# Moving the z projection of two images into the first image's scan, with a round trip through DRAM

## The chip, the cores and the metric

The kernel runs on one core of a Trainium2 chip. The metric is the device time of one execution in microseconds (us). The engines are named as in the profile: PE (TensorE, with PEld for its weight loads), DVE (VectorE), ACT (ScalarE), POOL (GpSimd), and SP, whose queue issues nearly all DMAs.

## The reference

Four layers work on `x` of shape (4 images, 384 channels, 48 x 48). Each is `x + layer(group_norm(x))`. Layer 0 is a state-space block, and it is the one that the change is about:

```python
xz = xs @ in_proj_w.T                      # 2304 tokens of an image, 384 -> 2 x 768
xin, z = jnp.split(xz, 2, axis=-1)
xin = silu(causal_conv4(xin) + conv_b)
dt, Bm, Cm = split(xin @ x_proj_w.T)       # 24, 16, 16
dt = softplus(dt @ dt_proj_w.T + dt_proj_b)
h = exp(dt * A) * h_prev + dt * B * x      # for each of 768 channels and 16 states
y = (sum over states of h * C + xin * D) * silu(z)
out = layer_norm(y @ out_proj_w.T)
```

Layer 1 is a projection, an 8 x 8 spectral filter, a depthwise 3 x 3 convolution and a gated projection; layer 2 a depthwise 11 x 11 convolution built from 4 points; layer 3 a mixture of 4 experts with a gate.

## The kernel before, in words

**Tiles.** Layer 0 runs image by image (b = 0 to 3), and an image's 2304 tokens in 5 chunks of 460 or 464 (t). So there are 20 chunks `i`. Channels lie on the 128 partitions: 384 are 3 tiles, 768 are 6 (m or j). A chunk has 96 (channel tile, state) pairs, and each is one **slot** `u`: 1920 slots in all. In each slot ACT makes `da = exp(dt * A)` in PSUM (`decay`, L821), POOL makes `bu = u * B` (`drive`, L832), DVE runs the scan along the tokens (L845), DVE or POOL multiplies by C (L865 or L874: in image 0 one slot in three is POOL's, later every other pair), and PE adds the result into a PSUM bank by a transposing matmul (`turned`, L770). ACT copies the scan's last column into `carry` (L859) for the next chunk. B and C rows come from DRAM, spread over all partitions, by two DMAs for every second slot, on SP's queue, in rings of 3 and 4 buffers; `drive` runs 3 slots ahead of the scan and `decay` 2.

**The work beside the scan.** The order of instructions on each engine is written out by this loop. Other work is cut into tasks, Python generators that yield the engine of their next step; a `Lane` advances each of its active tasks by at most one step when it comes by (once for ACT steps and once for the others in each slot; after an ACT step the task waits for the next slot). A task starts when the tasks it needs have ended, and a lane's queue is first in, first out. A `Meter` adds up the PE time that tasks announce: a slot takes 2.3 us off it and adds 0.44 for its own transposes, and while it stands above 2.0 a bound lane starts no step with a weight.

- Lane `aux` (not bound) holds layer 0's own tasks, put there for each chunk by `plan`: output projection (`out`, L916) and layer norm of the chunk before; `project_z` (six tasks j, L674 and L682, from slot 30 of the chunk); `project` for the next chunk (L642, L655, L661); `gates`, the Silu of `xc` and `z` in one go (slot 64); `steps` (dt); the image's group norm for the next image: `image_stats` (loads of half a channel tile and three `bn_stats` each, L573, in the first three chunks), `image_norm`, and `fold` (loads `w_inx` or `w_inz`, scales its rows by 1/std on ACT, and makes the mean's contribution on PE, L598).
- Lane `one` holds layers 1 to 3's routing scores of the image before (`later`, from slot 42 of an image on), and lane `two` the experts of that image (`experts`, L1602, 64 blocks of two products for an image), which need the last task of `later`. So image 0's scan has neither beside it. What is left after the scans runs in a tail: `later` of image 3, the rest of the experts, the routing and all experts of image 3 (L1702, L1719).

**z.** `project_z(i, j)` multiplies the chunk's `x` by the folded `w_inz` into a PSUM bank of the ring `mm` (3 banks), and ACT adds the bias and writes `zs[:, j]` (one buffer for all six j). `gates` applies Silu, `gate` (L902) multiplies y into it, and `out_proj` reads it.

**PSUM.** 8 banks: `mm` 3, `y` 2, `da` 2, `acc` 1. The bank `acc` is used by layers 1 and 2 only, so image 0's scan does not use it.

The functions that the diff touches:

Of the kernel before, what the change touches and what calls it, by code (L numbers as in the profile page):

```python
# [16 lines left out]
P = 128  # L17
NB, C, H, W = 4, 384, 48, 48
HW = H * W
# [114 lines left out]
def wait(slots):  # L134
    for _ in range(slots):
        yield ("pool",)
# [3 lines left out]
def tile_layers(ctx: ExitStack, tc: tile.TileContext, a: dict, out: bass.AP):  # L140
# [272 lines left out]
    with ExitStack() as first:  # L413
# [138 lines left out]
        def now(steps):  # L552
            for _ in steps:
                pass

        def scans(wk, mm, ring, meter, place, lanes, begin):
# [23 lines left out]


            def fold(b, which):
                w = (w_inx, w_inz)[which]
# [82 lines left out]
            def project_z(i, j):  # L666
                (b, t), c = G[i], st[i]
                n, d = CHUNKS[t], batch[b]
                yield ("pe", 2.3, (ring, 1))
                if "zs" not in c:  # L670
# [145 lines left out]
            def decay(u):  # L816
                i, p, m, s, _ = where(u)
                (b, t), c = G[i], st[i]
                n = CHUNKS[t]
                da = live["da", u] = mm.tile([P, 512], F32, name=f"da{b}_{t}_{m}_{s}", tag="da")  # L820
                nc.scalar.activation(  # L821
                    da[:, :n], c["dt", p][:, m % 2, :n], AF.Exp, scale=a_neg[:, m, s : s + 1]
                )
# [151 lines left out]

            aux = Lane(1 << 30, meter, bound=False)
            named = {}

            def plan(i, at):
# [3 lines left out]
                def put(q, name, make, *needs):  # L983
                    task = Task(make, [named[k] for k in needs if k in named], at + q)
                    named[name] = task
                    todo.append((q, task))
# [14 lines left out]
                if i < len(G):  # L1001
# [23 lines left out]
                    if b + 1 < NB:  # L1025
                        if t < CT:
                            put(43, ("stats", b, t, 0), lambda: image_stats(b + 1, t, 0), *rest)
                            put(66, ("stats", b, t, 1), lambda: image_stats(b + 1, t, 1),
                                ("stats", b, t, 0))
                        if t == CT:  # L1030
                            put(48, ("mean", b + 1), lambda: image_norm(b + 1))
                            put(70, ("fold", b + 1, 0), lambda: fold(b + 1, 0),
                                ("mean", b + 1), *done)
                        if t == CT + 1:
                            put(54, ("fold", b + 1, 1), lambda: fold(b + 1, 1), *done[:MT])
                aux.queue.extend(task for _, task in sorted(todo, key=lambda x: x[0]))

            def ready(u):
# [3 lines left out]
                while task and not task.ended:  # L1042
# [4 lines left out]
                    assert n < 1000, "stuck"  # L1047

            now(fold(0, 0))
            now(fold(0, 1))  # L1050
# [7 lines left out]
            with tc.manual_schedule():  # L1058
# [6 lines left out]
                spread(3, 0)  # L1065
                for u in range(2):
                    decay(u)
                for u in range(N + 6):
                    if u % LEN == 0 and u <= N:
                        plan(u // LEN, u)  # L1070
                    if u < N and u % (LEN * NC) == 42 and u > 42:
                        begin(G[u // LEN][0])
                    place[0] = u
                    for lane in (aux, *lanes):
                        lane.step(True, u)
# [7 lines left out]
                    meter.slot(0.44)  # L1083
                    early = u % PAIR >= 8
                    if early:
                        add(u - 5, True)
                        add(u - 3, False)
                    for lane in (aux, *lanes):
                        lane.step(False, u)
                    if u < N:  # L1090
                        product_now(u)
                    if u + 2 < N:
                        decay(u + 2)
                    if 0 < u <= N:
                        product(u - 1)
                    if u + 3 < N:
                        ready(u + 3)
                        drive(u + 3)
                    if not early:
                        add(u - 5, True)  # L1100
                        add(u - 3, False)
# [835 lines left out]
```

## Time and profile before

| what | value |
|---|---|
| median of 4 runs (lowest, highest) | 5428.84 us (5424.33, 5430.86) |
| the profiled execution's own time | 5433.5 us |
| its span (first to last instruction) | 5431.6 us |
| busy: PE, DVE, ACT, POOL | 4670.4, 4056.4, 2986.5, 3364.1 us |
| mean granted clock of PE | 0.912 |
| scan of image 0 (slots 0 to 479) | 89 to 1025 us |
| scan of image 1, 2, 3 | to 2140, to 3350, to 4528 us |
| tail | 4528 to 5432 us |
| chunk 0 to 4 | 179, 190, 188, 192, 187 us |
| chunk 14, chunk 19 (the last of images 2 and 3) | 221, 213 us |
| POOL's waits for B or C from DRAM: image 0, 1, 2, 3 | none listed, 8, 21, 25 us |

The borders of the scans are the starts of the 1st, 481st, 961st and 1441st scan instruction (L845). "Busy" is the union of an engine's instructions; an fp32 matmul shows as two records, so z's 18 matmuls of a chunk column block (6 groups j of 3) make 36 records. A wait line reads: who waited, for whom, us in total, how often, longest.

### The profile page before, as it was taken

How to read it: one execution, taken by the hardware profiler on the slowest of the kernel's cores; microseconds unless marked ns; L12 is line 12 of the kernel's file. 1: busy time of each engine (PE TensorE's matmuls, PEld its weight loads, DVE VectorE, ACT ScalarE, POOL GpSimd, SP SyncE). 2: the span in 40 equal slices, each digit the busy share in tenths (PEclk: the TensorE clock that was granted, in tenths of full speed). 3: DMA queues.
4: the chain of work that ended last, by engine and by line, in shares of the span. 5: the costliest groups of instructions: out<-in, count | busy, mean ns of one | idle time of the engine just before them, and what ended most of it. 6: DMA issues, size and time to landing. Idle time of an engine off the chain costs nothing. (4 is left out here: it accounts for less than half of the span.)

```text
span 5431.6 us, 81808 instructions
## 1 busy us (share of the span) xinstructions
PE 4670.4 (86%) x27796; PEld 3680.4 (68%) x27796; DVE 4056.4 (75%) x5581; ACT 2986.5 (55%) x6632; POOL 3364.1 (62%) x3020
## 2 busy tenths in 40 slices
PE   5677677687678989988889999988899999999899
PEld 3445455454447777665668887765678878889799
DVE  5989989888998888899887778899977774452200
ACT  3555565565558755655467655655576753334321
POOL 3878778876678788766667678776777673000000
PEclk8887788798789999999899999999999999999899
DMA  4444444454345555644555556554556554543200
GB/s 121 137 138 142 125 130 144 125 154 128 107 128 148 147 156 169 174 147 141 153 166 172 152 165 179 156 148 135 171 159 170 159 170 147 161 140 113 63 27 23
DMA packets 628392, 758.95 MB, mean 140 GB/s; under 512 B 58870, under 2 KB 622182, under 8 KB 627583
## 3 DMA queue, kind: packets, MB, share of 16 engines
q1 hardware_dynamic: 617668, 751.98, 47.5%
q8 instruction: 221, 3.62, 0.3%
q10 hardware_dynamic: 10298, 1.67, 0.2%
q14 instruction: 205, 1.67, 0.1%
HBM read 663.81 MB, written 89.65 MB: 139 GB/s over the span
## 5 line engine op out<-in xcount | busy, mean ns | idle before, releaser
L832 POOL TENSOR_TENSOR bu<-u,B 128x460 f32<-128x460 f32 (+1 forms) x1920 | 2224.9, 1168 | 809.5 <-DVE g L845 422.2
L821 ACT ACTIVATE da<-dt,a_neg 128x460 f32<-128x460 f32 (+1 forms) x1920 | 1242.9, 649 | 288.9 <-DVE g L865 185.0
L770 PE MATMUL y<-ident,g 128*115 128x128 f32 (+1 forms) x7680 | 1145.4, 298 | 272.4 <-DVE g L865 166.0
L770 PEld LDWEIGHTS y<-ident,g 128*115 128x115 f32 (+1 forms) x7680 | 1015.5, 187 | 500.1 <-DVE g L865 200.8
L874 POOL TENSOR_TENSOR g<-g,C 128x460 f32<-128x460 f32 (+1 forms) x885 | 1030.8, 1165 | 249.9 <-ACT carry L859 237.6
L845 DVE TENSOR_TENSOR_SCAN da<-da,carry,bu 128x460 f32<-128x460 f32 (+1 forms) x828 | 971.6, 1173 | 123.1 <-ACT da L821 95.3
L845 DVE TENSOR_TENSOR_SCAN g<-da,carry,bu 128x460 f32<-128x460 f32 (+1 forms) x708 | 820.0, 1167 | 106.0 <-ACT da L821 41.7
L865 DVE TENSOR_TENSOR g<-da,C 128x460 f32<-128x460 f32 (+1 forms) x1035 | 654.1, 632 | 89.5 <-PE y L770 28.5
L859 ACT COPY carry<-da 128x1 f32<-128x1 f32 x828 | 130.6, 158 | 834.3 <-DVE g L865 831.2
L1602 PE MATMUL pout<-hr,we 128*128 128x144 f32 x3456 | 484.7, 296 | 40.9 <-ACT hr L1618 30.8
L1602 PEld LDWEIGHTS pout<-hr,we 128*128 128x128 f32 x3456 | 456.3, 197 | 64.2 <-ACT hr L1618 41.7
L1602 PE MATMUL ph<-xe,we 128*128 128x144 f32 x3456 | 473.2, 292 | 12.8 <-DMA xe<-x3d 6.9
L1602 PEld LDWEIGHTS ph<-xe,we 128*128 128x128 f32 x3456 | 449.9, 195 | 29.5 <-issue 9.3
L1409 PE MATMUL pc<-band,row 128*128 128x162 f32 (+14 forms) x3456 | 457.0, 286 | 6.3 <-ACT row L1396 6.0
L1409 PEld LDWEIGHTS pc<-band,row 128*128 128x128 f32 x3456 | 444.3, 196 | 11.3 <-ACT row L1396 7.5
L1267 DVE SCALAR_TENSOR_TENSOR dw<-pad,w_dw,dw 128x384 f32<-128x384 f32 x576 | 347.7, 615 | 17.6 <-ACT pad L1242 6.7
L642 PE MATMUL pin<-xch,w_inx 128*128 128x463 f32 (+2 forms) x720 | 327.6, 595 | 33.6 <-DMA xch<-in_x 14.9
L1618 ACT ACTIVATE hr<-ph,nb 128x144 f32<-128x144 f32 x576 | 176.7, 377 | 306.3 <-PE ph L1602 304.7
L916 PE MATMUL po<-w_out,zs 128*115 128x384 f32 (+1 forms) x960 | 338.9, 496 | 6.9 <-DVE dt L750 6.4
L674 PE MATMUL pinz<-xch,w_inz 128*128 128x460 f32 (+1 forms) x720 | 317.8, 579 | 0.0
L1376 ACT ACTIVATE rep<-x,br,wr 128x192 f32<-128x192 f32 x576 | 274.1, 540 | 4.2 <-issue 4.2
L661 DVE SCALAR_TENSOR_TENSOR xc<-pin,conv_w,xc 128x460 f32<-128x460 f32 (+1 forms) x360 | 249.1, 692 | 30.6 <-ACT xc L655 21.1
(202 smaller groups left out, 5795.1 us busy)
## 6 DMA issues: line engine op xcount, KB each, us to landing
B<-bcd SPq DMA_DIRECT2D x768, 230.0 KB, 3.5
C<-bcd SPq DMA_DIRECT2D x768, 230.0 KB, 3.7
B<-bcd SPq DMA_DIRECT2D x192, 232.0 KB, 3.6
C<-bcd SPq DMA_DIRECT2D x192, 232.0 KB, 4.0
xe<-x3d SPq DMA_DIRECT2D x192, 216.0 KB, 2.8
ye<-y3d SPq DMA_DIRECT2D x144, 216.0 KB, 2.7
y3d<-ye SPq DMA_DIRECT2D x96, 216.0 KB, 2.2
xs<-x1d SPq DMA_DIRECT2D x24, 576.0 KB, 5.1
```

Source lines behind the costliest of these rows:

```text
L642: nc.tensor.matmul(ps[:, lo : halo + n], lhsT=w_inx[:, k, bass.ts(j, P)], rhs=c["x"][:, k, lo : halo + n], start=k == 0, stop=k == CT - 1,)
L674: nc.tensor.matmul(ps[:, :n], lhsT=w_inz[:, k, bass.ts(j, P)], rhs=c["x"][:, k, DCONV - 1 : DCONV - 1 + n], start=k == 0, stop=k == CT - 1,)
L770: nc.tensor.matmul(c["y", m][:w, bass.ts(k, P)], lhsT=src[:, bass.ts(k, w)], rhs=ident, is_transpose=True, start=c["terms", m] == 1 and k ...
L821: nc.scalar.activation(da[:, :n], c["dt", p][:, m % 2, :n], AF.Exp, scale=a_neg[:, m, s : s + 1])
L832: nc.gpsimd.tensor_mul(bu[:, :n], c["u", p][:, m % 2, :n], live["B", u // 2][:, :n])
L845: nc.vector.tensor_tensor_scan(here[:, :n], da[:, :n], bu[:, :n], last if t else nil[:, 0:1], ALU.mult, ALU.add,)
L865: nc.vector.tensor_mul(live["g", u][:, :n], live["h", u][:, :n], live["C", u // 2][:, :n])
L874: nc.gpsimd.tensor_mul(g[:, :n], g[:, :n], live["C", u // 2][:, :n])
L916: nc.tensor.matmul(ps[:w, :C], lhsT=c["zs"][:, m, bass.ts(k, w)], rhs=w_out0[:, m, :], start=m == 0, stop=m == MT - 1,)
L1267: nc.vector.scalar_tensor_tensor(v, src, w_dw[:, ct, k : k + 1], v, ALU.mult, ALU.add)
L1409: nc.tensor.matmul(d["acc2"][0][:, : BANDS[k] * W].rearrange("p (h w) -> p h w", w=W)[:, lo - edges[k] : hi - edges[k], xlo:xhi], lhsT=d[" ...
L1602: nc.tensor.matmul(ps[:, bass.ts(m, EB)], lhsT=w[:, k, bass.ts(m, P)], rhs=of[:, k, :], start=k == 0, stop=k == CT - 1,)
```

## The change

For the images 3 and 2 (`EARLY`), z is no longer projected in their own scans. A fourth lane, `start`, is bound by the meter and steps after `aux` in image 0's scan. Its tasks load x of both images once for the statistics (12 loads of half a channel tile, two buffers) and make their group norms; then for each image they fold a copy of the z weights in a buffer of their own, load x chunk by chunk (two buffers), and make z of one (chunk, j) after the other: three matmuls, an Identity with bias on ACT, and a store to DRAM (`zd`) from a ring of three buffers. In the scans of images 2 and 3, `project_z` issues one DMA that fetches the chunk's z (768 x 460 values) into `zs`, at j = 0, and makes no matmul. `image_stats`, `image_norm` and the fold of `w_inz` for these images are no longer planned in images 1 and 2; the fold of `w_inx` stays. The buffers of the lane live in a pool that is closed at the end of image 0's scan.

Besides, in image 0 every third slot's `da` takes the bank `acc`, so that there are three banks, and `decay` runs three slots ahead there. (The flag `early` of the loop is renamed `soon`.)

The diff, without `early_tasks` (which puts the tasks in the order of the text, each z needing the z before it) and without unchanged lines:

```diff
+            def early_stats(b, ct, h):
+                yield ("pool", 0, (early["xs"], 1))
+                t, k = early["xs"].take(f"xs0_{b}_{ct}_{h}")
+                half = HW // 2
+                nc.sync.dma_start(t, a["x"][b, bass.ts(ct, P), bass.ts(h, half)])
+                yield from wait(4)
+                st = early["stats", b]
+                for k3 in range(3):
+                    yield ("dve",)
+                    nc.vector.bn_stats(st[:, ct, h, k3, :], t[:, bass.ts(k3, LB)])
+                early["xs"].done(k)
...
+            def early_fold(b):
+                yield ("pool", 0, (early["w"], 1))
+                w, early["k", b] = early["w"].take(f"w_z{b}")
+                early["w", b] = w
+                nc.sync.dma_start(w, per_channel(a["L0_in_proj_wT"])[:, :, DI:])
+                yield from wait(4)
+                for k in range(CT):
+                    yield ("act",)
+                    nc.scalar.activation(
+                        w[:, k, :], w[:, k, :], AF.Copy, scale=rstd0[:, b, k : k + 1]
+                    )
+                yield ("pe", 2.0, (ring, 1))
...
+            def early_load(b, t):
+                yield ("pool", 0, (early["x"], 1))
+                x, _ = early["x", b, t] = early["x"].take(f"xz{b}_{t}")
+                cols = bass.ds(starts[t], CHUNKS[t])
+                nc.sync.dma_start(x[:, :, : CHUNKS[t]], strip(a["x"][b], cols))
+                yield from wait(4)
+
+            def early_z(b, t, j):
+                n = CHUNKS[t]
+                x, xk = early["x", b, t]
+                yield ("pe", 2.3, (ring, 1), lambda: early["z"].free())
+                ps, r = ring.take(f"pz{b}_{t}_{j}")
+                z, zk = early["z"].take(f"z{b}_{t}_{j}")
+                for k in range(CT):
+                    nc.tensor.matmul(
+                        ps[:, :n],
+                        lhsT=early["w", b][:, k, bass.ts(j, P)],
+                        rhs=x[:, k, :n],
+                        start=k == 0,
+                        stop=k == CT - 1,
+                    )
...
+                yield ("act",)
+                nc.scalar.activation(
+                    z[:, :n], ps[:, :n], AF.Identity, bias=early["nz", b][:, j : j + 1]
+                )
+                ring.done(r)
+                yield ("pool",)
+                nc.sync.dma_start(zd[b][bass.ts(j, P), bass.ds(starts[t], n)], z[:, :n])
+                early["z"].done(zk)
...
             def project_z(i, j):
                 (b, t), c = G[i], st[i]
                 n, d = CHUNKS[t], batch[b]
+                if b in EARLY:
+                    if j == 0:
+                        c["zs"] = wk.tile([P, MT, TM], F32, name=f"zs{b}_{t}", tag="zs", bufs=1)
+                        nc.sync.dma_start(
+                            c["zs"][:, :, :n],
+                            zd[b].rearrange("(m p) t -> p m t", p=P)[:, :, bass.ds(starts[t], n)],
+                        )
+                    yield from wait(5)
+                    return
...
-                da = live["da", u] = mm.tile([P, 512], F32, name=f"da{b}_{t}_{m}_{s}", tag="da")
+                spare = i < NC and u % 3 == 2
+                da = live["da", u] = mm.tile(
+                    [P, 512], F32, name=f"da{b}_{t}_{m}_{s}", tag="acc" if spare else "da",
+                    bufs=1 if spare else 2,
+                )
...
+            EARLY = (3, 2)
...
-                        if t < CT:
+                        if t < CT and b + 1 not in EARLY:
...
+                        if t == CT and b + 1 not in EARLY:
+                            put(48, ("mean", b + 1), lambda: image_norm(b + 1))
                         if t == CT:
-                            put(48, ("mean", b + 1), lambda: image_norm(b + 1))
                             put(70, ("fold", b + 1, 0), lambda: fold(b + 1, 0),
                                 ("mean", b + 1), *done)
-                        if t == CT + 1:
+                        if t == CT + 1 and b + 1 not in EARLY:
                             put(54, ("fold", b + 1, 1), lambda: fold(b + 1, 1), *done[:MT])
...
+            for tag, shape, n in (
+                ("xs", [P, HW // 2], 2), ("w", [P, CT, DI], 1), ("x", [P, CT, TM], 2),
+                ("z", [P, TM], 3),
+            ):
...
+            start = Lane(4, meter)
+            start.queue += early_tasks()
...
-                for u in range(2):
+                for u in range(3):
                     decay(u)
+                decays = 3
                 for u in range(N + 6):
+                    if u == LEN * NC:
+                        start.drain(u)
+                        first_image.close()
...
-                    for lane in (aux, *lanes):
+                    for lane in (aux, start, *lanes):
                         lane.step(True, u)
...
-                    if u + 2 < N:
-                        decay(u + 2)
+                    if decays < N and decays <= u + (3 if decays < LEN * NC else 2):
+                        decay(decays)
+                        decays += 1
```

## Prediction

> **What bounds the kernel now.** I read the page first (busy shares, then its second part), then the windows view over the stages, cut where the scan line L845 has run 480, 960, 1440 and 1920 times, then windows over thirds of a chunk (32 slots), then the waits of VectorE. The windows by stage (columns: window, its length, then busy us and instructions of PE, PEld, DVE, ACT and POOL, clock, DMA share, GB/s):
>
> ```profile
> 89.00:1025.00 936.00, 667.39 (x2960) 453.93 (x2960) 847.32 (x1035) 536.67 (x1122) 771.73 (x685) 0.80 0.46 135
> 1025.00:2140.00 1115.00, 911.12 (x4778) 654.99 (x4779) 972.72 (x1289) 683.93 (x1470) 861.13 (x774) 0.87 0.47 141
> 2140.00:3350.00 1210.00, 1097.93 (x6757) 870.94 (x6756) 997.45 (x1359) 734.07 (x1641) 863.25 (x772) 0.95 0.56 161
> 3350.00:4528.00 1178.00, 1085.63 (x6799) 873.99 (x6799) 976.09 (x1319) 720.94 (x1631) 858.39 (x768) 0.95 0.56 161
> 4528.00:4957.00 429.00, 413.36 (x2813) 360.88 (x2813) 182.18 (x368) 129.01 (x316) 5.85 (x15) 0.99 0.48 140
> ```
>
> Image 0 (first row) is VectorE's: 847 of 936 us busy, PE 667, at a clock of 0.80. In images 2 and 3 PE leads (0.91 and 0.92 of the stage) and the tail is PE's alone (413 of 429). So z moves from where PE is full to where PE has 269 us idle but VectorE has only 89.
>
> The same view by thirds: image 0's chunk 2, then chunk 9 (image 1, no experts beside it), then thirds of chunks 14, 15 and 19:
>
> ```profile
> 458.00:514.00 56.00, 42.28 (x204) 30.13 (x204) 53.44 (x68) 33.05 (x79) 51.93 (x48) 0.89 0.47 133
> 514.00:584.00 70.00, 50.33 (x216) 31.24 (x216) 65.62 (x83) 39.39 (x90) 53.04 (x47) 0.89 0.49 146
> 584.00:646.00 62.00, 39.85 (x168) 28.55 (x168) 52.10 (x62) 37.57 (x77) 49.27 (x45) 0.67 0.43 125
> 1941.00:2001.00 60.00, 55.80 (x346) 44.63 (x344) 55.69 (x75) 32.48 (x57) 57.39 (x53) 0.94 0.50 144
> 2072.00:2141.00 69.00, 59.90 (x407) 51.58 (x406) 54.75 (x74) 39.18 (x65) 57.02 (x51) 0.90 0.56 163
> 3129.00:3204.00 75.00, 74.89 (x539) 65.32 (x538) 56.96 (x72) 48.16 (x99) 59.39 (x54) 1.00 0.56 159
> 3350.00:3416.00 66.00, 65.39 (x438) 55.48 (x438) 55.91 (x81) 37.44 (x98) 57.65 (x53) 0.99 0.54 148
> 3416.00:3493.00 77.00, 73.70 (x424) 55.74 (x423) 68.17 (x99) 45.18 (x106) 59.62 (x56) 0.96 0.62 176
> 4316.00:4392.00 76.00, 75.90 (x541) 65.93 (x540) 55.47 (x70) 45.83 (x95) 58.71 (x53) 1.00 0.58 164
> ```
>
> With VectorE at 53 to 57 us a third takes 56 us when PE has 42, 66 when it has 65, and 75 when it has 75: the longer of the two engines plus a little. That is my ruler below.
>
> **Image 0: statistics.** 12 loads bring 36 bn_stats into image 0. The group line for the 18 that image 1 needs, which stay:
>
> ```profile
> L573 DVE BATCH_NORM_STATS2 stats<-xs 128x6 f32<-128x384 f32 x18 | 9.6, 534 | 0.0
> ```
>
> 36 x 0.534 = 19 us, plus two group norms of about 2 us on VectorE, in thirds where it is 94% busy: +23 at full price. The folds' 18 products (5.8 us of PE for 36 records, L598) only change stage.
>
> **Image 0: z.** A group (j) is 6 records. PE is busy 74.6 us for 30 groups in image 2, so 2.49 us each; image 0's own chunks take 84.7 for 30, 2.82 at its lower clock. Each group takes steps pe, act and pool in three successive slots and needs the group before it ended, and each chunk adds some 3 slots for its load: 60 groups in about 210 slots, 6.6 thirds, 9 groups (22.4 us of PE) a third. PE's thirds go from 42, 50, 40 to 65, 73, 62; the ruler says 66 instead of 56, 77 instead of 70, 69 instead of 62: +24 per chunk. PE's 42, 50 and 40 were measured at clocks of 0.89, 0.89 and 0.67, and thirds with more PE work show 0.90 to 1.00, so I take three quarters, 18: x 2.2 chunks = +40. Bounds: 0, if VectorE covers it all (PE below VectorE in each third at full clock, nearly so); and, at 2.82 us, PE thirds of 68, 76, 65, hence 69, 78, 70 us, +29 x 2.2 = +64.
>
> The Trainium skill, "TensorE: Matmul & The Clock Gate", Part 1 (The HAM clock gate), says that the clock is throttled by default and released by some 3.4 us of sustained work. The rows agree as far as they go (0.67 at a PE share of 0.64, 1.00 at 1.00). By the rule in full PE's old work would shrink to 38, 45, 27 us a third and z would cost some 26 instead of 40, which would make the total 14 us lower; no row here has z beside an otherwise empty lane, so I do not use it.
>
> What stands in line: on ACT, 60 Identity of 0.636 us wait for PE, and behind them on ACT's queue wait the carry copies and the decays that VectorE's scan needs. On PE the transposes of g wait behind z; g's 6 buffers give three slots. On SP 94 DMAs are added (12 + 2 + 10 loads, 60 stores, 10 fetches) and 14 removed (12 statistics loads, two w_inz); each store is issued a slot after its Identity, so SP, which the B and C spreads need, should wait little. POOL gets two small pow.
>
> **Image 0: third bank.** The waits of VectorE in image 0:
>
> ```profile
> DVE g L845 <- ACT carry L859: 22.4, 4, 5.6
> DVE g L845 <- ACT da L821: 6.4, 2, 5.3
> DVE da L845 <- ACT da L821: 4.5, 8, 0.8
> DVE dt L750 <- ACT carry L859: 4.3, 7, 0.7
> ```
>
> 37.6 us waiting for ACT, mostly 5 us once a chunk, behind the two Silu. The bank lets ACT be one slot (1.95 us) further ahead: some 2 us of each of 5 long waits and the few small ones, -12. Bounds 0 and -38. It cannot lose: decay(u+3) now waits for the product of slot u, as decay(u+2) did. Image 0: 23 + 40 - 12 = **+51**, between +11 (z hidden) and +87 (no gain from the bank, z at 64).
>
> **Images 1 and 2: statistics gone.** 9.6 + 2 us of VectorE each. Image 1's VectorE is 0.87 busy: -8; image 2's 0.82, in chunks 10 to 12: -5. Bounds 0 and -12 each.
>
> **Images 2, 3 and tail: z gone.** PE loses 74.6 + 77.6 = 152 us. But a slot cannot become shorter than VectorE allows, about 1.8 to 2.2 us, so what comes off depends on what fills the hole. The meter gives z's weight (2.3) to the expert blocks (4.4; 155.2 + 143.9 us of L1602 for 59 blocks in image 2, 5.07 us each): 14.9 / 5.07 = 2.9 blocks more per chunk. Images 2 and 3 now end their 64 blocks at 3314 and 4511 us, just before their scans end, and the next ones need the last task of `later`, whose score copies (L1523) run to 3329 and 4497. That chain takes a fixed number of slots: it ends at slot 64 of its last chunk in image 1 without experts, at 84 and 76 with them. So the blocks run out 12 or more early, and the last chunk of each image runs without them. Chunk 14: 75 to 60 as in the chunk 9 row, its second third 78 to 69, the last unchanged, and 5 at the end of chunk 13: -29. Chunk 19: 76 to 60 and 74 to 62: -28. Some 6 blocks of the tail get into the end of image 3: 30 us of PE, of which I take 22, because the end of the 4528 to 4957 stretch is a group norm chain. Together -79. If the holes are not refilled, chunks 10, 13, 14, 15, 18, 19, where PE is 0.92 busy or more, lose 15 each and the four VectorE-bound ones 5 each: -110. All of it would be -152; the two last chunks alone -57. I take **-90**, near the refilled case, since the meter decides and it is soft.
>
> **The fetch.** 10 DMAs of 1,380 KB, 34 slots (80 us) ahead of Silu: hidden itself. What follows on SP's queue is at stake: B issued 0.4 us behind a 690 KB x load (2232 us) landed in 5.2 us instead of 3.5. A load of 1,152 KB alone lands in 8.4. So B behind the fetch lands in some 7; it is issued about 5 slots (12 us) before POOL reads it. Bounds -10 (the removed loads were in B's way too) and +40 (4 us each); I take +8.
>
> The Trainium skill, "DMA: Bandwidth & Descriptors", section Queues, rings and completion order, speaks against the fetch: each ring is consumed in order. In full that would make B land after about 8.4 + 3.5 = 12 us, an estimate from this trace's landings; that is just the 12 us of lead, and the sum would move towards +40 only beyond it. The measured 5.2 shows part of it.
>
> **Sum.** 51 - 8 - 5 - 90 + 8 = -44. The profiled execution took 5433.5 us (its span 5431.6 and about 2 around it), which is 4.7 above the median of 5428.84; I take the same difference off the median: **5385**.
>
> **Rivals.** (B) PE's 152 us come off whole, since experts always fill: 51 - 13 - 152 + 8 = -106, 5323. For it: PE 0.96 busy in the tail, to which work would have to be pulled up; against: `later` blocks the next experts. (C) Slower: in image 0 each z group costs VectorE a slot, because its Identity waits for PE on ACT ahead of carry and decay: 23 - 12 + 60 x 1.95 = 128, so 128 - 13 - 90 + 8 = +33, 5462. It turns the sign from (103 - 8 - 11) / 60 = 1.4 us a group. For it: VectorE idles only 89 us in 936 and 37.6 of them on ACT; against: images 2 and 3 have such Identities, PE nearly full, and wait for da only 36 and 64 us. (D) The change does not do what it says: PE's gain dies behind VectorE everywhere but in the two last chunks: 51 - 13 - 57 + 8 = -11, 5418.
>
> **Numbers.** Forecast 0.50, B 0.20, C 0.22, D 0.08. Forecast and D together reach from 5345 to 5425. The corners are 11 - 24 - 152 - 10 = -175 (5254) and 87 - 57 + 40 = +70 (5499); about one in ten beyond each end leaves 5305 to 5470. A measurement of this kernel tells 0.2% (11 us) from no change: faster 0.68, same 0.08, slower 0.24.
>
> **What would show it.** Image 0 at about 987 us with the clock near 0.9; waits for ACT da below 11 us. Chunks 14 and 19 near 195 and 185 us instead of 221 and 213, experts ended a chunk earlier; a tail of about 880. Wrong, if image 0 exceeds 1065 us (C), if the tail loses 60 us or more (B), if POOL waits for B far beyond today's 16 and 21 us in images 2 and 3, or if z is not over by two thirds of image 0.

## The result, and the profile after

| | before | after |
|---|---|---|
| median (lowest, highest) of the runs | 5429.62 us (5418.71, 5446.89), 66 runs | 5438.75 us (5423.93, 5454.56), 45 runs |
| ratio to before, with its 95% interval | | 1.0013 [1.0008, 1.0018] |
| profiled execution, its span | 5433.5, 5431.6 us | 5432.07, 5430.2 us |
| scan of image 0, 1, 2, 3 | 936, 1115, 1210, 1178 us | 961, 1109, 1214, 1179 us |
| tail | 903 us | 881 us |
| PE busy in images 2 and 3, and the tail | 1098, 1086, 861 us | 1054, 1031, 835 us |

The change costs 0.13%, some 7 us: within the 0.2% that I called no change, and far from the 44 us of gain that I forecast. Single executions of one kernel scatter by 10 to 15 us around its median (the lowest and highest of the first row), so I read sizes of a few us from the ratios of many runs, and places from the traces. The traces of before and after differ by 1.4 us in all where the ratio says 7.

First the windows by stage of after, as in the prediction (window, length, then busy us and instructions of PE, PEld, DVE, ACT and POOL, clock, DMA share, GB/s):

```profile
86.00:1047.00 961.00, 782.52 (x3440) 514.03 (x3440) 864.77 (x1092) 572.66 (x1188) 775.07 (x689) 0.86 0.54 163
1047.00:2156.00 1109.00, 914.67 (x4826) 657.39 (x4827) 962.36 (x1272) 684.17 (x1475) 861.34 (x772) 0.88 0.47 138
2156.00:3370.00 1214.00, 1054.27 (x6635) 861.15 (x6634) 996.63 (x1340) 718.28 (x1617) 862.21 (x771) 0.92 0.57 164
3370.00:4549.00 1179.00, 1030.93 (x6624) 851.89 (x6623) 976.59 (x1320) 704.61 (x1602) 857.64 (x768) 0.94 0.58 167
4549.00:4950.00 401.00, 386.07 (x2582) 334.15 (x2580) 176.01 (x346) 119.36 (x290) 4.19 (x14) 0.98 0.49 144
```

Image 0 got 25 us longer with 115 us more of PE in it; the tail got 22 us shorter. The third and fourth rows are the riddle: PE is 44 and 55 us less busy, VectorE has what it had, and neither scan is shorter. PE's share fell from 0.91 and 0.92 to 0.87. So another thing now ends last there.

The same view by thirds of a chunk: image 0's chunk 2, the first third of chunk 14, the first two of chunk 15, and the first of chunk 19:

```profile
480.00:539.00 59.00, 55.08 (x238) 35.41 (x239) 53.19 (x68) 36.68 (x87) 51.69 (x47) 0.94 0.58 183
539.00:607.00 68.00, 66.65 (x284) 40.79 (x283) 64.96 (x82) 44.83 (x98) 52.85 (x48) 1.00 0.62 190
607.00:671.00 64.00, 51.74 (x215) 31.22 (x214) 53.12 (x64) 42.10 (x86) 50.46 (x45) 0.82 0.54 169
```

```profile
3158.00:3231.00 73.00, 59.12 (x385) 49.25 (x384) 64.60 (x78) 34.26 (x62) 58.71 (x53) 0.89 0.46 142
3370.00:3437.00 67.00, 64.93 (x439) 55.26 (x437) 55.99 (x83) 37.72 (x98) 57.70 (x53) 0.99 0.56 158
3437.00:3524.00 87.00, 67.75 (x387) 54.60 (x388) 66.16 (x96) 43.11 (x102) 58.57 (x55) 0.84 0.63 188
4355.00:4425.00 70.00, 63.52 (x434) 53.34 (x433) 56.99 (x79) 37.07 (x70) 56.69 (x52) 0.94 0.45 133
```

In image 0 the thirds took 59, 68 and 64 us where they took 56, 70 and 62 before, although PE does up to 16 us more in each, at a higher clock. Chunk 15's second third (the third row of the second fence) is the clearest loss: 87 us against 77, with PE at 68 of them and VectorE at 66. Neither is full. My ruler, "the longer of the two plus a little", would say 69.

By chunks, chunk 19 went from 213 to 193 us and chunk 14 from 221 to 211, as far as the direction goes; but chunks 10 (228 to 236), 13 (241 to 254), 15 (225 to 236) and 17 (234 to 243) gave it back.

What ended the waits in images 2 and 3 (who waited, for whom, us in total, how often, longest): VectorE's for C and SP's own, first of before, then of after:

```profile
DVE g L865 <- DMA C<-bcd: 5.2, 5, 1.5
```

```profile
SPq L1592 <- DMA y3d<-ye: 149.8, 64, 6.1
SPq L1589 <- DMA y3d<-xe: 102.1, 28, 7.3
```

```profile
DVE g L983 <- DMA C<-bcd: 48.6, 15, 9.3
```

```profile
SPq L1735 <- DMA y3d<-ye: 171.4, 64, 6.2
...
SPq L1732 <- DMA y3d<-xe: 135.0, 31, 8.7
```

The product with C waited 5 us for its rows and now waits 49. SP itself stands still at the experts' loads: a load into `xe` or `ye` (L1732, L1735) reuses a buffer whose content is still on its way to DRAM, and what follows on SP is issued behind it. It did so before the change too, for 252 us, and now for 306. (At the same loads it stands another 63 us before and 75 after, where the store goes to `out`.) What that does is seen best in one place, SP and then VectorE in chunk 15 of after (start, us, instruction; on VectorE the idle time before it and its releaser):

```profile
3479.13 0.37 SPq L1786 DMA_DIRECT2D y3d<-xe  x1
3486.62 0.37 SPq L1732 DMA_DIRECT2D xe<-x3d  x1
3487.03 0.48 SPq L1735 DMA_DIRECT2D ye<-y3d  x1
3487.61 0.44 SPq L927 DMA_DIRECT2D B<-bcd  x1
3488.10 0.42 SPq L927 DMA_DIRECT2D C<-bcd  x1
```

```profile
3493.32 0.64 DVE L983 TENSOR_TENSOR g<-da,C 128x460 f32<-128x460 f32 x1 [3.81 <-DMA C<-bcd]
```

SP issues the store of `xe` at 3479.1. The next instruction on SP is the load into the same `xe`, and it goes at 3486.6, when the store has landed: 7.1 us with nothing issued. The B and C of the coming slots stand behind it, go at once when it is over, and VectorE waits 3.8 us for C.

### The profile page after: what moved, and what is told of

It reads as the page before. It is cut to its first block, busy times and chain, and to the rows that moved or that the text cites. A ratio compares the mean times of both kernels' runs of the same rounds, so it can differ in the third digit from the quotient of the medians.

```text
span 5430.2 us, 81921 instructions
## 1 busy us (share of the span) xinstructions
PE 4663.7 (86%) x27796; PEld 3684.2 (68%) x27796; DVE 4057.5 (75%) x5581; ACT 2985.2 (55%) x6632; POOL 3364.0 (62%) x3020
## 5 line engine op out<-in xcount | busy, mean ns | idle before, releaser
L883 PE MATMUL y<-ident,g 128*115 128x128 f32 (+1 forms) x7680 | 1114.3, 293 | 203.7 <-DVE g L983 121.7
L883 PEld LDWEIGHTS y<-ident,g 128*115 128x115 f32 (+1 forms) x7680 | 997.0, 184 | 423.2 <-DVE g L983 145.4
L1745 PE MATMUL ph<-xe,we 128*128 128x144 f32 x3456 | 485.7, 297 | 33.1 <-DMA xe<-x3d 16.4
L963 DVE TENSOR_TENSOR_SCAN da<-da,nil,bu 128x460 f32<-128x460 f32 x207 | 242.4, 1171 | 31.0 <-ACT da L939 20.0
```

Source lines behind the costliest of these rows:

```text
L883: nc.tensor.matmul(c["y", m][:w, bass.ts(k, P)], lhsT=src[:, bass.ts(k, w)], rhs=ident, is_transpose=True, start=c["terms", m] == 1 and k ...
L963: nc.vector.tensor_tensor_scan(here[:, :n], da[:, :n], bu[:, :n], last if t else nil[:, 0:1], ALU.mult, ALU.add,)
L1745: nc.tensor.matmul(ps[:, bass.ts(m, EB)], lhsT=w[:, k, bass.ts(m, P)], rhs=of[:, k, :], start=k == 0, stop=k == CT - 1,)
```

## The experiments

All ratios are to the kernel before, with their 95% intervals; 0.1% is 5.4 us. "Trace" means stage lengths in one profiled execution. The letters in the expectations stand for theories: F, that the fetch is what costs; R, that SP's queue, held at loads whose buffer is still being stored, is what costs; S, that the pace of the expert blocks is; C, in the expectation of e9, that more bytes in flight make the rows late, whoever issues them (not the rival C of the prediction). P and L are two theories of what z's removal is worth in the scans, told where they are used. A kernel with `memset` in place of z computes with z at 0.5; where it says so, that part of the computation is left out.

### Image 0's three parts

**The bank alone (e5_bank_alone): before, with the third `da` bank and nothing else.**

```diff
+                spare = i < NC and u % 3 == 2
+                da = live["da", u] = mm.tile(..., tag="acc" if spare else "da", ...)
...
-                    if u + 2 < N:
-                        decay(u + 2)
+                    if decays < N and decays <= u + (3 if decays < LEN * NC else 2):
+                        decay(decays)
+                        decays += 1
```

> The kernel before with the third decay bank alone. The prediction gave it 12 us; the waits after Silu of image 0 (5.6 us in each of 5 chunks before, 4.5 with the bank in the changed kernel) speak for 5 to 8: ratio 0.9985 to 0.999. If the bank only pays because z's Identity stands on ACT in image 0 (taking it away from the changed kernel cost 0.3%), it is 1.000 here.

Measured 0.9986 [0.9975, 0.9996], some -8 us; image 0 went from 936.2 to 932.9 us in the trace. The bank gains, a little less than the 12 that I took.

**After without the bank (e4_two_banks).**

```diff
-                spare = i < NC and u % 3 == 2
+                spare = False
...
-                for u in range(3):
+                for u in range(2):
                     decay(u)
-                decays = 3
+                decays = 2
...
-                    if decays < N and decays <= u + (3 if decays < LEN * NC else 2):
+                    if decays < N and decays <= u + 2:
```

> The changed kernel without its third decay bank (decay runs two slots ahead everywhere, the bank acc is not used in image 0). The prediction gave the bank 12 us, bounds 0 and 38. The traces show the wait after the Silu of each chunk of image 0 at 5.6 us before and 4.5 after, which speaks for some 6 us in all: ratio about 1.0025. If the bank is what hides z's Identity on ACT in image 0 (z cost there 5 us instead of the forecast 40), image 0 gets longer by 20 to 40 us: ratio 1.005 to 1.009.

Measured 1.0045 [1.0031, 1.0059]; image 0 took 969.2 us instead of 960.8. Beside the Identity instructions of z the bank seems worth more than alone: 8 us in image 0's trace, some 17 by the ratios (1.0045 less 1.0013), where alone it was 3 and 8; the intervals of the ratios do not quite separate the two.

**The statistics alone (e8_stats_moved_alone): after, with z and the fold of `w_inz` put back into images 2 and 3.** The group norms of both images stay in image 0, and so does the bank.

```diff
-                for b in EARLY:
-                    fold_ = put(lambda b=b: early_fold(b), norms[b])
...
-                if b in EARLY:
...
-                    yield from wait(5)
-                    return
...
-                        if t == CT + 1 and b + 1 not in EARLY:
+                        if t == CT + 1:
```

> The changed kernel with z where it was: only the statistics of images 3 and 2 are made in image 0's scan, with the third bank there; z and the folds of w_inz are in images 2 and 3 as in the kernel before, nothing is stored or fetched. The prediction's terms give +23 for the statistics, -8 and -5 in images 1 and 2, and for the bank -12 (or -5 to -8 by the traces): about +2 us, ratio 0.9995 to 1.001; image 0's first chunk 22 us longer, its others 1 to 3 us shorter.

Measured 1.0024 [1.0015, 1.0033]. Against e5, which lacks just the moved statistics, that is 0.38% or 21 us of loss. In the traces image 0 takes 950.3 instead of 932.9 us, +17.4 (I forecast +23), but images 1 and 2 together give back nothing: -5.0 and +4.0 where I forecast -8 and -5. And after has image 0 at 960.8, 10.5 more than e8: that is the price of all 60 z groups there, which I put at 40.

### The fetch

**No fetch (e1_no_fetch): after, z's six parts set to 0.5 on POOL in place of the fetch, so that silu(z) is left out in images 2 and 3.**

```diff
                         c["zs"] = wk.tile([P, MT, TM], F32, name=f"zs{b}_{t}", tag="zs", bufs=1)
-                        nc.sync.dma_start(c["zs"][:, :, :n], ...)
+                    nc.gpsimd.memset(c["zs"][:, j, :n], 0.5)
```

> The changed kernel without the fetch of z: in the scans of images 2 and 3, six memsets on POOL (460 elements each, one per z task) fill zs with 0.5 in place of the DMA of 1,380 KB, so the output for these images lacks the true z. Theory F (the fetch in one piece delays the C and B rows behind it on SP's queue, some 50 us of waits of VectorE for C in images 2 and 3): those waits go and the time falls to about 5385 us, ratio to before about 0.992. Theory R (the expert blocks that take the place of z in slots 30 to 54 block SP's queue themselves, by loads that wait for the stores of the same buffer; the fetch is innocent): the waits stay, ratio 1.000 to 1.003. The memsets cost POOL some 60 x 0.5 us where it is 0.72 busy, at most 10 us of the time.

Measured 0.9988 [0.9979, 0.9997], so the fetch is worth 0.25%, some 14 us, and not the 52 us that theory F needs to be the whole of what is missing. F falls; 14 is between my 8 and my upper bound of 40. R is not met in full either: it had the waits stay, and in the middle thirds VectorE's waits for DMA fall from 46 to 23 us (table below).

**The fetch in six (e2_fetch_in_six): after, one DMA of 230 KB per z task instead of one of 1,380 KB.**

```diff
-                        nc.sync.dma_start(c["zs"][:, :, :n], zd[b]...)
+                    nc.sync.dma_start(
+                        c["zs"][:, j, :n], zd[b][bass.ts(j, P), bass.ds(starts[t], n)]
+                    )
```

> The changed kernel with the fetch cut in six DMAs of 230 KB, one per z task, 4 slots apart. Theory F: each piece delays a row by under 2 us, which the lead of 5 slots hides; waits for C fall from 52 us to under 15, time about 5390 us, ratio 0.993. Theory R: unchanged, 1.001.

Measured 0.9998 [0.9988, 1.0008], 8 us better than after. The size of the one DMA is part of its price, but VectorE's waits for DMA in the middle thirds stay as they were (table below).

### What z is worth in images 2 and 3

**After, with z's weight kept (e3_weight_kept):** the z tasks still announce 2.3 us to the meter, so that the expert blocks do not take z's place.

```diff
+                    yield ("pe", 2.3)
                     yield from wait(5)
                     return
```

> The changed kernel, where each z task of images 2 and 3 still announces its PE weight of 2.3 to the meter without issuing a matmul, so that the expert blocks keep their old places; the fetch stays in one piece. Theory F: the waits for C stay near 50 us; PE's 152 us come off the scans as far as VectorE lets them (-110), image 0 +25, image 1 -7: ratio about 0.992, with the tail as before (903 us). Theory R: the waits for C go as well, ratio about 0.983.

Measured 1.0015 [1.0004, 1.0026]: no gain, and both theories missed. The tail is back at 903 us, image 3 at 1165 instead of 1179: what the blocks do not take from the scan they keep in the tail. R had expected the waits for C to go when the blocks stay in their old places. They do not; in images 2 and 3 they are 38 us (5 before, 49 in after):

```profile
DVE g L984 <- DMA C<-bcd: 23.8, 8, 7.0
```

```profile
DVE g L984 <- DMA C<-bcd: 13.7, 7, 7.2
```

So the rows come late also without blocks in z's place.

**Before, with z left out of images 2 and 3 (e6_no_z_in_2_3), nothing added elsewhere,** and **the same with the weight kept (e7_no_z_weight_kept).** Both leave out z's matmuls and Identity there and compute with 0.5.

```diff
+                if b >= 2:
+                    if j == 0:
+                        c["zs"] = wk.tile([P, MT, TM], F32, name=f"zs{b}_{t}", tag="zs", bufs=1)
+                    nc.gpsimd.memset(c["zs"][:, j, :n], 0.5)
+                    yield from wait(5)
+                    return
```

and in e7 one line more, ahead of the `memset`:

```diff
+                    yield ("pe", 2.3)
```

> The kernel before without z's projection in images 2 and 3: matmuls, Identity and meter weight are left out, six memsets on POOL per chunk fill zs with 0.5; nothing is added in image 0 and nothing is fetched. The output for these images lacks the true z. This is the whole gain that the move could bring in images 2, 3 and the tail. Theory P (the prediction's step: a third of a chunk lasts as long as the longer of PE and VectorE): 79 to 110 us less, ratio 0.980 to 0.985. Theory L (the scans of images 2 and 3 are not PE's although it is 0.91 busy there: taken off, PE's time turns into PE's idle time and a lower clock, and only the tail gains): 20 us in the tail and 10 to 20 in the scans, ratio 0.993 to 0.995.

> As the kernel without z in images 2 and 3, but each z task still announces its 2.3 us to the meter, so that no expert block moves up and the tail stays at 903 us. Theory P: PE's 152 us come off the scans as far as VectorE lets them, about 100 us, ratio 0.980. Theory L: 10 to 30 us, ratio 0.994 to 0.998.

Measured 0.9960 [0.9946, 0.9974] and 0.9951 [0.9937, 0.9965]: -22 and -27 us. This is the main finding against my forecast. Taking 150 us of PE away with no statistics, no fetch and no z in image 0 is worth only 22 to 27 us, by either pace. With the kernel's queues as they are, the gain is not there even where nothing is added: P falls, and L is the nearer, though e6 gains less than it said. In e6's trace it is the tail's 23 us alone (880.2 instead of 903.0); the scans of images 2 and 3 take 1208.6 and 1186.6 us, where they took 1209.6 and 1178.4:

```profile
2143.00:3351.00 1208.00, 1074.12 (x6802) 878.35 (x6803) 1003.74 (x1376) 720.98 (x1629) 875.43 (x802) 0.94 0.58 163
3351.00:4538.00 1187.00, 1039.77 (x6630) 860.26 (x6629) 979.82 (x1321) 705.36 (x1604) 869.44 (x798) 0.93 0.58 160
```

Two cautions go with these traces. In the session of e5 to e8 before itself ran at 5438 us, 9 more than in the table of results, so a stage of e6 or e7 set beside the trace of before looks a little too long. And e7's profiled execution, 5432.8 us, was the slowest of its six, 16 us above their median: its trace does not show where the 27 us were gained.

What came in PE's place, counted from the traces: VectorE's idle time (gaps of 0.2 us and more) in the ten middle thirds of images 2 and 3, where z used to run, by what ended it.

| us of VectorE idle, ended by | ACT | PE | DMA | POOL |
|---|---|---|---|---|
| before | 34 | 43 | 3 | 5 |
| after | 22 | 23 | 46 | 4 |
| e1, no fetch | 25 | 26 | 23 | 8 |
| e2, fetch in six | 24 | 23 | 42 | 7 |
| e6, z left out | 26 | 20 | 34 | 9 |
| e7, left out, weight kept | 22 | 31 | 12 | 5 |

PE's and ACT's waits fall by 32 us, as they should when z goes, and waits for DMA take their place: +42 in after, and +30 in e6, which has no fetch at all. In e6 the C rows are late too, and SP stands at the same loads (these lines end 23 us before image 3 does; to its end the last one is 141 us):

```profile
DVE g L871 <- DMA C<-bcd: 40.0, 14, 8.7
```

```profile
SPq L1598 <- DMA y3d<-ye: 167.9, 64, 7.3
SPq L1595 <- DMA y3d<-xe: 128.8, 31, 6.3
```

With the weight kept (e7) DMA is not it, and still little is gained. The middle third of chunk 10, before and in e7:

```profile
2207.00:2285.00 78.00, 71.55 (x412) 52.82 (x412) 68.30 (x103) 45.76 (x107) 60.33 (x57) 0.98 0.63 186
```

```profile
2209.00:2290.00 81.00, 65.48 (x364) 50.74 (x364) 68.61 (x104) 41.74 (x100) 62.67 (x63) 0.87 0.61 180
```

PE has 48 records fewer, 30 of them z's and 18 of an expert block, some 15 us in all, but is only 6 us less busy, at a clock of 0.87 instead of 0.98; VectorE's 68 us stay. Over the ten middle thirds PE's busy time falls from 760 to 668 us and VectorE's stays (714 and 718); their length goes from 816 to 801 us. So where z used to run VectorE is nearly as full as PE, and with z gone it has 0.90 of the time.

### The queue

**After, with the buffer given back later (e9_store_lands_first):** an expert block reports its buffer free two slots after it has issued the store, so that the planner starts the block that loads into it later.

```diff
                 nc.sync.dma_start(strip(out[b] if e == NE - 1 else y3d, bass.ts(s, EB)), x)
+                yield from wait(2)
                 done(key)
```

> The changed kernel, where an expert block hands its buffer back two slots after its store is issued, so that the next load into it is issued when the store has landed and does not hold SP's queue. Theory R (the expert blocks that moved into the z slots hold SP's queue, and the B and C rows behind them come late): SP's waits for y3d and out stores (193 us in image 2) fall below 60, VectorE's waits for DMAs in the middle thirds of images 2 and 3 from 46 us to below 20, ratio about 0.997. Theory C (the rows are late because more bytes are in flight in these slots, whoever issues them): SP waits less, but the waits for C stay, ratio about 1.001. If blocks become slower and slip into the tail (5 us each), the tail shows it.

Measured **0.9932 [0.9918, 0.9946]**, 5388.85 us against 5426.58 in the same session: 37 us faster than before, and faster than both kernels of the case. This is nearly the time that I forecast for the change as it was, and more gain than either theory had expected here. Theory C falls: the rows come in time. Its waits of VectorE and of SP in images 2 and 3, and its stages:

```profile
DVE g L983 <- DMA C<-bcd: 3.9, 3, 1.7
```

```profile
SPq L1732 <- DMA y3d<-xe: 46.8, 24, 5.0
SPq L1735 <- DMA y3d<-ye: 46.7, 31, 4.6
```

```profile
1046.00:2149.00 1103.00, 902.95 (x4781) 649.22 (x4782) 960.68 (x1268) 684.26 (x1472) 860.53 (x773) 0.89 0.47 139
2149.00:3327.00 1178.00, 1046.32 (x6649) 851.96 (x6648) 992.33 (x1340) 718.80 (x1617) 861.99 (x771) 0.94 0.58 169
3327.00:4507.00 1180.00, 1031.17 (x6615) 849.67 (x6614) 980.87 (x1320) 705.32 (x1601) 858.06 (x769) 0.94 0.57 167
```

SP's waits for the `y3d` stores fell from 306 to 94 us (88 without the first 15 us of the tail, which these lines include), C's from 49 to 4, and image 2 takes 1178 us instead of 1214. Image 3 does not get shorter.

**The same pace with SP held (e12_store_two_slots_later):** the two slots lie ahead of the store, and the buffer is free at once. In the traces the blocks stand where they stand in e9: of 192 blocks 186 begin their first activation (`hr`) in the same slot, the other six one slot apart, and both have 59 in the tail (after has 58, before 64). Only the store's landing is in SP's way again.

```diff
                 yield ("pool",)
+                yield from wait(2)
                 nc.sync.dma_start(strip(out[b] if e == NE - 1 else y3d, bass.ts(s, EB)), x)
```

> The control to the version that waits two slots between an expert block's store and the reuse of its buffer (0.9932): here the two slots stand ahead of the store, and the buffer is handed back at once as in the changed kernel. The blocks are paced as there, but the next load again follows its buffer's store at once and holds SP's queue until the store has landed. Theory R (SP's queue held): SP's waits for y3d stores come back (150 us in image 2), VectorE's waits for DMAs in the middle thirds of images 2 and 3 stay near 46 us, ratio 0.998 to 1.002. Theory S (the gain came from the slower pace of the blocks, which spreads them to the ends of the images where PE idled): ratio 0.993 to 0.995 as there.

Measured 1.0003 [0.9988, 1.0018], 0.7% or 38 us above e9. So in sum it is the held queue, and the pace (S) falls: by itself it is worth some 5 us against after. By images it is less even: e12 is 24 us shorter than after in image 2 and 29 longer in image 3. The waits of VectorE and of SP in images 2 and 3, and the stages, of e12:

```profile
DVE g L983 <- DMA C<-bcd: 31.4, 11, 7.1
```

```profile
SPq L1735 <- DMA y3d<-ye: 237.0, 64, 8.3
SPq L1732 <- DMA y3d<-xe: 129.2, 29, 7.9
```

```profile
2150.00:3340.00 1190.00, 1051.66 (x6654) 858.37 (x6654) 991.90 (x1340) 717.92 (x1618) 863.00 (x772) 0.94 0.58 167
3340.00:4548.00 1208.00, 1045.88 (x6610) 860.85 (x6611) 980.26 (x1319) 703.59 (x1601) 858.99 (x768) 0.93 0.57 163
```

PE and VectorE have the work that they have in e9 to a few us (PE 15 in the second row), and the two scans take 12 and 28 us more. VectorE's waits for C explain 27 of the 40; in the middle thirds its idle time ended by DMA is 27 us here and 2 in e9.

**The two slots on before (e10_store_lands_first_before), and on before with the bank (e11_bank_store_lands_first).** The edit is e9's one line.

> The kernel before with the same two slots between store and reuse. There VectorE waits only some 10 us for DMAs in images 2 and 3, so by R and by C alike little is to be had: ratio 0.998 to 1.001, with SP's waits for the stores gone.

> The kernel before with the third bank (0.9986 alone) and the two slots between store and reuse: a version that could beat both kernels. Ratio 0.997 to 0.9995, the sum of the two parts.

Measured 1.0050 [1.0036, 1.0064] and 1.0038 [1.0024, 1.0052], both slower than expected. Where z is in the scans, the two slots cost: in e10's trace images 2 and 3 are 12 us shorter, but 9 blocks slip into the tail, which takes 946 instead of 903 us. So e9 is not an improvement that any version of the kernel would have had; it needs the room that z left.

**e9 without the fetch (e13_lands_first_no_fetch):** e9's line and e1's together, z at 0.5 in images 2 and 3.

```diff
-                        nc.sync.dma_start(c["zs"][:, :, :n], ...)
+                    nc.gpsimd.memset(c["zs"][:, j, :n], 0.5)
...
+                yield from wait(2)
                 done(key)
```

> The version at 0.9932 without the fetch of z (six memsets on POOL per chunk in its place; the output of images 2 and 3 lacks the true z). Without the fetch the changed kernel was 13 us faster (0.9988 against 1.0013). If the fetch costs by what it adds to a queue that is held anyway, it costs next to nothing here: ratio 0.992 to 0.994. If its bytes cost by themselves: ratio 0.990 to 0.991.

Measured 0.9940 [0.9917, 0.9963], against 0.9932 with the fetch: nothing that can be told. So the fetch's 14 us were most likely not a price of its own but the held queue's; the two intervals together still allow it some 10 us.

## Why the prediction was wrong, by its own steps

The term of the sum that failed is "Images 2, 3 and tail: z gone", my -90. Beside it, what each term came to by the runs:

| term | forecast | measured | from |
|---|---|---|---|
| third bank | -12 | -8 | e5 |
| statistics, all images | 23 - 8 - 5 = +10 | +21 | e8 against e5 |
| z in image 0 | +40 | +10 | traces of after and e8 |
| fetch | +8 | +14 | after against e1 |
| z gone | -90 | -22, -27; -30 as the rest | e6, e7; after against e8, less the two rows above |
| sum | -44 | +7 | after 1.0013 |

**z gone.** The tail did what I said: -22 forecast, -22 in the trace. The scans did not: -68 forecast, +5 in the trace. I read the stage with a ruler of two engines, took a third to last as long as the longer of PE and VectorE, and let experts refill the holes for free. The ruler left out SP's queue, on which the B and C rows stand behind loads that wait for stores. Before the change SP stood there for 252 us of images 2 and 3 too, with VectorE's C in time but for 5 us: the wait was in the profile, and cost nothing. In the runs without z there it reaches VectorE, with 19 us of waits for C in e7 up to 49 in after. That this is because the slots have become shorter of other waits is my reading and not shown; e8, with z in its place, has 19 us too. I had weighed a late B or C only as a consequence of the fetch, and e6 shows it without one. The refill is not what brought it, or only in part: only 6 blocks more than before lie ahead of the tail, and with the blocks kept in place VectorE still waits 38 us for C (e3). The fetch adds to it (29 us in e1, 49 in after).

That the held queue took much of the gain is shown by e9 against e12, same blocks in the same places, 38 us apart. Freed of it the change gains -37 where I forecast -44, but that the two are so near is luck. By the table's sum, -37 less -8, +21 and +10 leaves -60 for z gone (nothing taken for the fetch), and by the traces e9 is 30 us shorter than before in images 2 and 3 and 26 in the tail. So z gone is worth some -60 with SP freed and -30 with SP held, and not -90; the 30 that were still missing came back because z cost image 0 30 less than I took. (e9 against e11, which both have the two slots and the bank, gives some -89 for it by the same sum, but there the two slots cost e11 9 blocks in the tail.)

What else was wrong is in e7. Where z used to run VectorE is busy 714 of 816 us. Summed over these ten thirds, the longer of PE and VectorE falls only from 771 us (before) to 724 (e7), so that by the ruler itself 47 us could come off there, and 15 did. The second third of chunk 15 in my rows, at 77 us with VectorE at 68, could lose 9 at most, while my "not refilled, -110" took 15 off its chunk. Two more of my rows, 62 us with VectorE at 52 and 69 with PE at 60, already stood 9 and 10 us above the longer engine. And where no block refills, the clock falls with PE's load (e7: 0.87 for 0.98). No run that took only z away came near -110. Which of these holds the last 30 us is not shown.

**z in image 0** cost 10 instead of 40. I took three quarters of the ruler's 24 us a chunk. The clock paid for much of it: thirds of 0.89, 0.89 and 0.67 became 0.94, 1.00 and 0.82, so that z and the old work together made PE 55, 67 and 52 us busy, where I had counted on 65, 73 and 62. ACT did wait more, as feared, 32 us for z's products, but VectorE's idle time ended by ACT did not grow (44 us before, 42 after). VectorE's waits in image 0 of after:

```profile
DVE da L963 <- ACT da L939: 17.9, 4, 4.5
...
DVE dt L863 <- ACT dt L860: 7.6, 6, 1.5
...
DVE da L963 <- ACT carry L977: 4.8, 2, 4.6
```

Waits for the carry, 22.4 us in the first line before, show 4.8, and those for `da`, which I wanted below 11, are 18. The long waits went in part from the one to the other. z was over by the end of chunk 2, earlier than my two thirds.

The Trainium skill, "TensorE: Matmul & The Clock Gate", Part 1 (The HAM clock gate), gave, with PE's old work taken at full clock, an estimate of 26 for z here instead of the 40 that I took. The measured 10 is on its side of my number: here the rule was the better guide, and I had set it aside because no row had z beside an emptier PE.

**Statistics.** 17 in image 0 against 23: right in kind. That images 1 and 2 would give 13 back did not come true in e8 (-5 and +4). Why is open.

**The fetch** was placed rightly between its bounds, but its price is hardly its own: 14 us with SP held, nothing that can be told without (e13). The Trainium skill, "DMA: Bandwidth & Descriptors", Queues, rings and completion order, which says that descriptors are consumed in ring order, is not refuted by this; but what held B and C in the rows above was one step earlier, SP not having issued them. The same page's section Issuing engines are not separate DMA queues calls the time that a sequencer spends on initiating a DMA usually small beside the DMA itself. In this case that of the initiation itself is (0.4 us a DMA in the rows above, against some 4 us to the landing of C), while the wait in front of it was 2.7 and 4.4 us in the mean of the two lines, up to 8.7, and was worth some 38 us in sum where it could be taken away (e12 against e9).

**The rivals.** D, that PE's gain dies in the scans, came nearest; I gave it 0.08 and the wrong place (VectorE alone, and a total of -11, since I still counted 57 us for the two last chunks, which gave 29). B falls: the tail lost 22 and not 60 us. C falls: image 0 is 961 us and z cost 0.2 us a group there, not 1.95. Of the four signs by which I wanted to see the forecast fail, one showed: POOL's waits for B rose from 16 and 21 us to 33 and 32. VectorE's wait for C, which tells the story, was not on the list.

**What stays open.** Why image 3 is no shorter in e9 than before (chunks 16 and 17 are longer by 9 and 16 us, 15 and 19 shorter by 10 and 8). Why images 1 and 2 give nothing back in e8. How much of e7's missing gain is the clock and how much VectorE. z left out of images 2 and 3 with the buffers given back later, which would bound the move with SP freed, was not run. Loads of the experts on another issuing engine, or a third `xe` buffer, were not tried.

## What to carry to other kernels

Before pricing work moved off a full engine, look what the other engines have in the same stretch, and follow the loop's loads through the queue that issues them: here expert loads held an in-order DMA queue before and after, and the engines' busy shares showed nothing of it. A wait in an issuing queue that costs nothing today can become a price when the slots get shorter; where the schedule has room for it, set a buffer's store and its next load apart in issue order, so that nobody stands behind the landing. And leave the work out altogether in one run first: that run (22 to 27 us for 150 us of PE) bounds what any way of moving it can gain in the schedule as it stands.

## What the runs showed of the hardware that was not expected

- Work put beside a PE that was 0.71 busy cost far less than its busy time: 60 groups with some 2.5 us of PE each, 150 us, cost image 0 10 us, while the granted clock rose from 0.80 to 0.86 over the stage and to 1.00 in the fullest third.
- The reverse showed too: 48 records (some 15 us) taken out of a third at a clock of 0.98 left PE 6 us less busy, at 0.87.
- A load whose buffer is still being stored holds SP until the store has landed, up to 8.7 us at a time, 306 us for the `y3d` stores in images 2 and 3 of after, and everything issued from SP stands behind it.
